# Two chained bottleneck blocks on one core: the column sums of the last stage spread over the units of a pair, a stream that takes no unit ahead, and one idle matmul more at two places of the Gram stages

## The chip, the cores and the metric

The kernel runs on one core of a Trainium2 chip. The metric is the time of one execution on the device in microseconds (us); less is better. In this text PE is TensorE, DVE is VectorE, ACT is ScalarE, POOL is GpSimd, and SP is SyncE, whose queue issues most of the DMAs.

## The reference

The input x is 64 images of 1024 channels and 14 x 14 pixels in float32. Two identical blocks follow each other. Each block computes

```
h = relu(bn1(conv1x1(x, w1) + b1))      # 1024 -> 256 channels
h = relu(bn2(conv3x3(h, w2) + b2))      # 256 -> 256
h = bn3(conv1x1(h, w3) + b3)            # 256 -> 1024
x = relu(x + softplus(residual_scale) * h)
```

where bn takes its mean and variance over all images and pixels. So no block can normalise before its whole convolution is done, and the work falls into stages.

## The kernel before, in words

**Stages.** In order of time the trace shows: the first 1x1 convolution (about 27 to 302 us), the 3x3 convolution of block 0 (302 to 592), the Gram stage of block 0 (from about 592), a fused stage that runs the last convolution of block 0 and the first of block 1 side by side (about 672 to 1270), the 3x3 convolution of block 1 (to 1562), its Gram stage (to about 1646), and the last stage (to the end at 1957.5), which is the last 1x1 convolution of block 1 with the residual sum, the relu and the output. In a Gram stage the variance of the third convolution is computed from the product of its input with itself, so that the convolution need not be run twice.

**Seven products.** A 1x1 convolution is done with seven products in place of eight for a 2 x 2 arrangement of weights and pixels. The class `Seven` names them `p1` to `p7`; behind each stands what is done with its result, `after1` to `after7`. They need four sums of the moving operand, `t1` to `t4`, and four of the weights. In the last stage a unit (`Conv3Pair`) is one choice q of 0 to 3 of output slots for two tiles of images, t and t + 1; four units make a pair of tiles, and there are 15 pairs (t = 1, 3, ..., 29). Each product there is one matmul call of 128x128 weights with 392 columns, which the trace shows as two instructions. The sums t1 to t4 depend on the pair only. They are the tiles `ct0` to `ct3`, made by `column_sums` (L423) in four DVE instructions: t3 (L430), t2 (L431, from t3), t1 (L432), t4 (L433, from t2). `ct0` and `ct1` (t1 and t2) have one buffer, `ct2` and `ct3` (t3 and t4) two.

**The order in a unit.** `stream` (L300) interleaves two units: p1 of the new unit, then p3 and p4 of the one before (`last`), then p6, p2, p5, p7 of the new one. After p2, p5, p3 and p4 DVE adds the scaled bank to the residual tile x (L466, banks named cx, cp, cp, cy). The bank cp that p5 starts is the same that p3 accumulates into, two products later, so p3 cannot start until the L466 after p5 has read the bank. After p1, p6 and p7 ACT saves the bank (L459, shown under its helper L333), and POOL adds these to x (L487, L513). `end` does three relus on ACT; `go_out` (L520) does the fourth relu on DVE (L522) and issues two output DMAs on SP (L525).

**The stream takes a unit ahead.** `stream` asks its generator for the following unit before it issues the present one. So what the generator does around a unit stands in the program one unit early: `go_out` of unit k - 2 and the loads of x (L123, behind unit q = 1 of a pair) stand ahead of unit k, and the column sums of the next pair stand ahead of unit q = 3 of the present one. The same `stream` serves the first stage (whose generator loads x) and the fused stage (loads of x and column sums).

**What sets the order on the engines.** Matmuls, ACT's instructions and some DVE instructions go through `tc.keep_in_program_order`, which pins an instruction behind the one that was traced last on its engine. The others are ordered when the program is built: each engine takes the earliest instruction in the program whose inputs and buffers are ready by a model. So an instruction that isn't pinned can be put ahead of its place in the program as soon as its buffer is free. L430 to L433 and L466 are not pinned; L522 is.

**Gram stages.** `conv2` ends with idle matmuls, `busy(psum, "m", 6)` (L968): matmuls with the identity of 448 columns into a bank that nobody reads. Behind them the Gram stage normalises the first pixels (ACT L546, DVE L552, L554, L994) and transposes them on PE in `by_tensor` (L1019, L1024).

Of the kernel before, what the change touches and what calls it, by code (L numbers as in the profile page):

```python
# [37 lines left out]
FP = mybir.dt.float32  # L38
# [3 lines left out]
P = 128  # L42
N, C, H, W = 64, 1024, 14, 14
HW = H * W
M = 256
CS = C // P
MS = M // P
G = 2
# [39 lines left out]
def bottlenecks(ctx: ExitStack, tc: tile.TileContext, x, w1s, w2s, w3s, pars, out):  # L88
# [14 lines left out]
    def two(t, s):  # L103

        j = t % (GI // G)
        return y_grp[:, s, t // (GI // G), :, j * G * W : (j + 1) * G * W]
# [63 lines left out]
    def busy(psum, tag, n, with_=None):  # L170

        v = ident if with_ is None else with_
        for i in range(n):
            matmul(psum.tile(448, tag), v, v[:, :1].to_broadcast([P, 448]), start=True, stop=True)
# [122 lines left out]
            yield from self.p3()  # L297
            yield from self.p4()

    def stream(items, beside=lambda: None):  # L300


        before, items = None, iter(items)
        now = next(items)
        while now is not None:
            following = next(items, None)
            yield from now.p1()
            if before is not None:
                beside()
                yield from before.last()  # L310
                beside()
            else:
                yield from now.p2()
            yield from now.p6()
            if before is not None:
                before.end()
                if following is not None:
                    beside()
                    yield from now.p2()
            beside()  # L320
            yield from now.p5()
            beside()
            yield from now.p7()
            beside()
            if following is None:
                yield from now.p2()
            before, now = now, following
        yield from before.last()
        before.end()

# [91 lines left out]

    def column_sums(pool, ys, n):  # L423

        sums = []
        for i in range(4):
            v = pool.tile([P, n], FP, tag=f"ct{i}", name=f"ct{i}", bufs=2 if i > 1 else 1)
            sums.append(v.rearrange("p (h l) -> p h l", l=G * W))
        t1, t2, t3, t4 = sums
        nc.vector.tensor_sub(t3, ys[1][1], ys[0][1])  # L430
        nc.vector.tensor_add(t2, t3, ys[0][0])  # L431
        nc.vector.tensor_sub(t1, ys[0][1], ys[0][0])  # L432
        nc.vector.tensor_sub(t4, ys[1][0], t2)  # L433
        return sums

    class Conv3(Seven):

# [118 lines left out]
    def conv2(psum, pool, b, par, aff, affine_of, stats):  # L556
# [395 lines left out]
        for k in range(NG * NF):  # L952
# [12 lines left out]
            item.columns(*qs)  # L965
            finished.send(item)
            queue = queue[1:] + list(itertools.islice(made, 1))
        busy(psum, "m", 6)  # L968

    def conv3(psum, t, o, w3, tag=None):  # L970
        ps = psum.tile(tag=tag)
# [6 lines left out]
    def gram(psum, pool, homes, aff, minus_c, beside):  # L978

        g0, g1 = psum.tile(M + 1, "cp"), psum.tile(P + 1, "ap")
        zts = [pool.tile([P, CH, M + 1], FP, tag=f"zt{i}", name=f"zt{i}") for i in range(NZT)]
        for zt in zts:
            nc.gpsimd.memset(zt[:, :, M:], 1.0)
        zts = itertools.cycle(zts)

        head = 3 * CH * P
        start = FIRST * CH * P
        bounds = [0, CH * P, head, head + STEP, *range(2 * GPX, NPX + 1, GPX)]  # L990
        pieces = list(zip(bounds, bounds[1:]))

        def less(s, y):
            tc.keep_in_program_order(nc.vector.tensor_scalar(y, y, minus_c[:, s : s + 1], None, ALU.add))  # L994

        def norm_to(end):

            while pieces and pieces[0][0] < end:
                a, e = pieces.pop(0)
                for s in reversed(range(MS)):  # L1000
                    y = y_all[:, s, a:e]
                    if a == 0 and s == 1:
                        norm_vector(s, y, aff, minus_c[:, s : s + 1])
                    else:
                        norm(s, y, aff)
                        less(s, y)

        def spread(k):

            first = start + k * STEP if k else head  # L1010
            norm_to(first + STEP)
            x = homes[k % 2][:, : MS * STEP].rearrange("p (s j f) -> p s j f", s=MS, j=4)
            for i, j in itertools.product(range(4), range(4)):
                queue = nc.gpsimd if 4 * i + j in (1, 3, 6, 8, 10, 13, 15) else nc.sync
                a = first + i * RUN
                queue.dma_start(out=x[32 * i : 32 * i + 32, :, j], in_=y_all[32 * j : 32 * j + 32, :, a : a + RUN])
            return x.rearrange("p s j f -> p (s j) f")

        def by_tensor(a):  # L1019
            tp = psum.tile(CH * M)  # L1020
            for c in range(CH):
                for s in range(MS):
                    tc.keep_in_program_order(
                        nc.tensor.transpose(  # L1024
                            tp[:, (c * MS + s) * P : (c * MS + s + 1) * P],
                            y_all[:, s, a + c * P : a + (c + 1) * P], ident,
                        )
                    )
            zt = next(zts)
            tc.keep_in_program_order(nc.vector.tensor_copy(zt[:, :, :M], tp.rearrange("p (c m) -> p c m", c=CH)))  # L1030
            return zt

        def by_vector(x, i):
            zt = next(zts)
            tc.keep_in_program_order(
                nc.vector.transpose(
                    zt[:, :, :M].rearrange("p b (n c) -> p b n c", c=32),
                    x[:, :, i * CH * 32 : (i + 1) * CH * 32].rearrange("p n (b r) -> p b n r", r=32),
                )
            )  # L1040
            return zt

        def pairs():

            norm_to(head)
            then = {
                1: lambda: ready.append(spread(0)),
                2: partial(norm_to, 2 * GPX),
                4: partial(norm_to, 3 * GPX),
                5: lambda: ready.append(spread(1)),  # L1050
            }
            for i in range(FIRST):
                a = i * CH * P
                yield by_tensor(a if a < head else a + STEP)
                if i in then:
                    then[i]()
            for k in range(STEPS):
                x = ready.pop(0)
                for i in range(RUN // (CH * 32)):
                    yield by_vector(x, i)  # L1060
                if k + 2 < STEPS:
                    ready.append(spread(k + 2))
            norm_to(NPX)
            for i in range(LAST):
                yield by_tensor(NPX - (LAST - i) * CH * P)

        ready = []
        total = NPX // (CH * P)
        before = None
        for k, zt in enumerate(itertools.chain(pairs(), (None,))):  # L1070
            if before is not None:
                for c in range(CH):
                    first, last = k == 1 and c == 0, k == total and c == CH - 1
                    matmul(g0, before[:, c, 0:P], before[:, c, :], start=first, stop=last)
                    matmul(g1, before[:, c, P:M], before[:, c, P:], start=first, stop=last)
            before = zt
            if k in beside:
                beside[k]()
        return g0, g1
# [61 lines left out]
    def final(psum, pool, xpool, xs, a, w3, aff):  # L1141


        units = []

        def pairs():
            for t in range(1, T - 1, 2):
                ys = [[two(t + i, s) for i in range(2)] for s in range(MS)]
                sums = column_sums(pool, ys, PX)
                for q in range(CS // 2):  # L1150
                    units.append(Conv3Pair(psum, pool, xs[t : t + 2], q, PX, ys, sums, w3, aff, out[t : t + 2]))
                    yield units[-1]

                    while len(units) > 2:
                        units.pop(0).go_out()
                    if q == 1:

                        for i in range(len(xs), min(t + 5, T)):
                            xs.append(load_x(xpool, 1, i))

        for _ in stream(pairs()):
            pass
        for unit in units:
            unit.go_out()
        residual(psum, xs[T - 1], 1, T - 1, a, aff)

    def fused(psum, pool, xpool, xs, w1, w3, aff, par, stats, one_done):
# [13 lines left out]
        def first_convs():  # L1181
            for t in range(T):
                yield Conv1(psum, pool, xs[t : t + 1], (t,), w1, par, stats, one_done)

        a, c = stream(first_convs()), stream(last_convs())
        for i in range(LAG):
            next(c)
        while True:
# [125 lines left out]
    with tc.tile_pool(name="first", bufs=1) as one, tc.tile_pool(  # L1314
# [32 lines left out]
                xs = [load_x(xpool, 0, t + i) for i in range(2)]  # L1347
                yield Conv1(psum, one, xs, (t, t + 1), w1, par[0], stats1, one_done)

        for _ in stream(items(), beside):  # L1350
            pass

    for b in range(2):
# [95 lines left out]
```

## Time and profile before

| | us |
|---|---|
| median of 3 runs | 1959.82 |
| lowest and highest | 1959.64, 1960.51 |
| profiled execution, whole | 1959.24 |
| its span, first to last instruction | 1957.5 |
| PE busy | 1919.9 (98%) |
| PEld busy | 1614.4 (82%) |
| DVE busy | 1552.4 (79%) |
| ACT busy | 1041.5 (53%) |
| POOL busy | 532.0 (27%) |
| DMA moved | 408.39 MB, 48.5% of 16 engines' time on SP's queue |

The busy times are summed over the whole span, whose stages have different limits, so a stage is read in a window of its own. A matmul's recorded length overlaps the next one's; the spacing of their starts is what PE needs. An instruction's line can be that of a helper (L168 for all matmuls, L333 for all pinned ACT instructions), so the tiles' names tell what it does. Between the span and the execution's time lie 1.74 us.

### The profile page before, as it was taken

The page shows a single profiled execution, that of the slowest core. Times are in us where ns is not written, and L with a number is a line of the kernel's source. Part 1 is how long each engine was busy: PE and PEld are TensorE (multiplying, and loading weights), DVE is VectorE, ACT ScalarE, POOL GpSimd, SP SyncE. Part 2 cuts the span into 40 slices and gives each one's busy share as a digit, 9 for nine tenths or more (in the row PEclk, how much of TensorE's full clock was granted, in tenths as well). Part 3 has the DMA queues.
Part 4 walks back from the last instruction along what each step waited for, and adds up shares of the span by engine and source line. Part 5 has one row for each costly group of instructions (what it writes and reads, how often), then busy time and mean ns, then how long its engine had stood idle before and what let it go on. Part 6 is the DMA issues. An engine that isn't in the chain of part 4 may idle for free.

```text
span 1957.5 us, 26989 instructions
## 1 busy us (share of the span) xinstructions
PE 1919.9 (98%) x9430; PEld 1614.4 (82%) x9430; DVE 1552.4 (79%) x2491; ACT 1041.5 (53%) x2082; POOL 532.0 (27%) x638
## 2 busy tenths in 40 slices
PE   9999999999999999999999999989999999999998
PEld 5555558999997799999999999989999887555554
DVE  5778768999998667676776776699999976888786
ACT  2222214677775055555555555457777641666665
POOL 0111100000105133433433333301010051666664
PEclk9999999999999999999999999999999999999999
DMA  7766635576747634444444444257667386899997
GB/s 289 278 248 254 249 112 165 178 208 191 207 142 203 198 135 187 173 165 177 182 169 165 179 184 166 99 183 204 203 192 207 124 199 232 298 322 339 336 341 264
DMA packets 188983, 408.39 MB, mean 209 GB/s; under 512 B 24944, under 2 KB 165136, under 8 KB 172336
## 3 DMA queue, kind: packets, MB, share of 16 engines
q1 hardware_dynamic: 161728, 324.66, 48.5%
q0 software_dynamic: 21504, 30.94, 6.9%
q10 hardware_dynamic: 5616, 51.06, 6.3%
q8 instruction: 75, 1.23, 0.3%
q14 instruction: 60, 0.49, 0.1%
HBM read 263.75 MB, written 115.34 MB: 194 GB/s over the span
## 4 chain that ended last, share of the span: by engine, by line
PE 90%; DVE 7%; issue 1%; ACT 1%; DMA 1%; SPq 0%; POOL 0%; DVEq 0%
PE ay L168 17%; PE cy L168 16%; PE columns L168 13%; PE cp L168 12%; PE ap L168 10%; PE m L168 6%; PE l L168 6%; PE ax L168 4%; PE cx L168 4%; PE ps L168 1%; DVE x L466 1%; DVE ct L431 1%; DVE f L801 0%; DMA home<-y 0%; DVE ct L433 0%
## 5 line engine op out<-in xcount | busy, mean ns | idle before, releaser
L333 ACT ACTIVATE cu<-cy,scale 128x196 f32<-128x196 f32 (+1 forms) x552 | 257.7, 473 | 286.7 <-PE cy L168 279.6
L168 PE MATMUL columns<-v,ub 128*128 128x224 f32 (+1 forms) x1536 | 301.1, 337 | 0.7 <-ACT columns L760 0.7
L168 PEld LDWEIGHTS columns<-v,ub 128*128 128x128 f32 x1536 | 269.4, 188 | 4.1 <-ACT columns L760 1.2
L333 ACT ACTIVATE x<-x,shift 128x392 f32<-128x392 f32 x428 | 239.7, 613 | 55.1 <-POOL x L492 53.2
L466 DVE SCALAR_TENSOR_TENSOR x<-cp,scale,x 128x196 f32<-128x196 f32 (+1 forms) x368 | 178.1, 484 | 98.0 <-PE cp L168 96.4
L168 PE MATMUL cy<-ct,ws 128*128 128x196 f32 (+1 forms) x736 | 222.0, 383 | 1.1 <-ACT cu L333 1.1
L168 PE MATMUL ay<-at,ws 128*128 128x196 f32 (+1 forms) x752 | 209.2, 381 | 0.0
L487 POOL TENSOR_TENSOR x<-x,cu 128x196 f32<-128x196 f32 (+1 forms) x184 | 159.2, 865 | 174.1 <-ACT cu L333 162.5
L492 POOL TENSOR_TENSOR x<-x,cu 128x392 f32<-128x392 f32 x124 | 125.9, 1015 | 192.8 <-DVE x L466 188.1
L168 PEld LDWEIGHTS ay<-at,ws 128*128 128x128 f32 x752 | 136.4, 190 | 33.6 <-ACT au L333 0.5
L168 PEld LDWEIGHTS cy<-ct,ws 128*128 128x128 f32 x736 | 133.4, 190 | 36.4 <-ACT cu L333 3.8
L168 PE MATMUL m<-sums,ua 128*128 128x224 f32 (+1 forms) x752 | 147.6, 340 | 6.2 <-DVE sums L624 6.2
L168 PE MATMUL l<-diffs,ub 128*128 128x224 f32 (+1 forms) x768 | 149.7, 338 | 3.0 <-PE columns L168 2.9
L513 POOL TENSOR_TENSOR x<-x,cu 128x392 f32<-128x392 f32 x120 | 124.5, 1038 | 86.1 <-DVE x L466 79.2
L871 POOL DMA_DIRECT2D y<-f x24 | 31.1, 1532 | 412.8 <-DVE f L801 320.8
L168 PEld LDWEIGHTS l<-diffs,ub 128*128 128x128 f32 x768 | 133.6, 189 | 7.0 <-PE columns L168 5.9
L168 PEld LDWEIGHTS m<-sums,ua 128*128 128x128 f32 x752 | 132.2, 191 | 8.7 <-DVE sums L624 7.9
L466 DVE SCALAR_TENSOR_TENSOR x<-cx,scale,x 128x196 f32<-128x196 f32 (+1 forms) x184 | 89.3, 485 | 59.1 <-PE cx L168 58.2
L333 ACT ACTIVATE au<-ay 128x196 f32<-128x196 f32 (+1 forms) x141 | 53.6, 380 | 152.0 <-PE ay L168 149.3
L168 PE MATMUL cx<-y,w 128*128 128x196 f32 (+1 forms) x404 | 124.1, 392 | 0.4 <-DVE x L1130 0.4
L168 PE MATMUL cy<-y,w 128*128 128x196 f32 (+1 forms) x404 | 123.8, 392 | 0.0
L168 PE MATMUL cp<-zt 128*128 128x257 f32 x392 | 118.8, 385 | 1.8 <-DVE zt L1030 1.7
(211 smaller groups left out, 3950.1 us busy)
## 6 DMA issues: line engine op xcount, KB each, us to landing
x<-in_x SPq DMA_DIRECT2D x62, 1568.0 KB, 6.8
ub<-u SPq DMA_DIRECT2D x94, 768.0 KB, 5.0
x<-mid SPq DMA_DIRECT2D x32, 1568.0 KB, 8.6
mid<-x ACTq DMA_DIRECT2D x31, 1568.0 KB, 5.1
out<-x SPq DMA_DIRECT2D x123, 392.0 KB, 6.5
ua<-u SPq DMA_DIRECT2D x94, 256.0 KB, 3.0
u<-y POOLq DMA_DIRECT2D x48, 256.0 KB, 5.9
home<-y SPq DMA_DIRECT2D x90, 96.0 KB, 4.2
```

What stands on the lines that cost most here:

```text
L168: tc.keep_in_program_order(nc.tensor.matmul(*args, **kw))
L333: tc.keep_in_program_order(nc.scalar.activation(*args, **kw))
L431: nc.vector.tensor_add(t2, t3, ys[0][0])
L466: nc.vector.scalar_tensor_tensor(v, bank, self.scale[:, o : o + 1], v, ALU.mult, ALU.add)
L487: nc.gpsimd.tensor_add(self.part(1, 1), self.part(1, 1), u3)
L492: nc.gpsimd.tensor_add(v, v, self.u12)
L513: nc.gpsimd.tensor_add(v, v, self.u12[:, i * self.n : (i + 1) * self.n])
L871: nc.gpsimd.dma_start(out=out_rows[0][:, o], in_=f[:, o], accum_op=ALU.add)
```

## The change

`stream` no longer asks for the following unit first; it is told the number of units, and takes each one when it is due. So everything that a generator does around a unit stands in the program behind the unit before it, one unit later than it did, in the first, the fused and the last stage.

In the last stage the four column sums are split from the allocation of their tiles (`sums_of`, `sum_steps`). The first pair's are made ahead of its units. Those of the next pair are made one at a time: t3 behind unit q = 0, t2 behind q = 1, t1 behind q = 2, t4 behind q = 3. All four tiles have two buffers there. `go_out` of unit k - 2 now stands behind the step of unit k, and the loads of x behind unit q = 1. The fused stage keeps `column_sums` and its buffers.

`conv2` ends with seven idle matmul calls instead of six, and one more stands behind the first `by_tensor` of each Gram stage, into the bank `ax`.

```
-        before, items = None, iter(items)
-        now = next(items)
-        while now is not None:
-            following = next(items, None)
+        before = None
+        for k, now in enumerate(items, 1):
             yield from now.p1()
...
-                if following is not None:
+                if k < total:
...
-            if following is None:
+            if k == total:
                 yield from now.p2()
-            before, now = now, following
+            before = now
...
+    def sums_of(pool, n, bufs=1):
+        tiles = [pool.tile([P, n], FP, tag=f"ct{i}", name=f"ct{i}", bufs=2 if i > 1 else bufs) for i in range(4)]
+        return [v.rearrange("p (h l) -> p h l", l=G * W) for v in tiles]
+    def sum_steps(ys, sums):
         t1, t2, t3, t4 = sums
+        return [
+            lambda: nc.vector.tensor_sub(t3, ys[1][1], ys[0][1]),
+            lambda: nc.vector.tensor_add(t2, t3, ys[0][0]),
+            lambda: nc.vector.tensor_sub(t1, ys[0][1], ys[0][0]),
+            lambda: nc.vector.tensor_sub(t4, ys[1][0], t2),
+        ]
...
-        busy(psum, "m", 6)
+        busy(psum, "m", 7)
...
                 yield by_tensor(a if a < head else a + STEP)
+                if i == 0:
+                    busy(psum, "ax", 1)
...
         def pairs():
+            def inputs(t):
+                ys = [[two(t + i, s) for i in range(2)] for s in range(MS)]
+                sums = sums_of(pool, PX, 2)
+                return ys, sums, sum_steps(ys, sums)
+            ys, sums, steps = inputs(1)
+            for step in steps:
+                step()
             for t in range(1, T - 1, 2):
-                ys = [[two(t + i, s) for i in range(2)] for s in range(MS)]
-                sums = column_sums(pool, ys, PX)
+                if t > 1:
+                    ys, sums, _ = following
+                following = inputs(t + 2) if t + 2 < T - 1 else None
                 for q in range(CS // 2):
                     units.append(Conv3Pair(psum, pool, xs[t : t + 2], q, PX, ys, sums, w3, aff, out[t : t + 2]))
                     yield units[-1]
+                    if following is not None:
+                        following[2][q]()
                     while len(units) > 2:
                         units.pop(0).go_out()
```

More of the change, by code (lines that the diff above doesn't have):

```diff
@@ L298, in last, with stream @@
             yield from self.p4()
-    def stream(items, beside=lambda: None):
-        before, items = None, iter(items)
-        now = next(items)
-        while now is not None:
-            following = next(items, None)
+    def stream(items, total, beside=lambda: None):
+        before = None
+        for k, now in enumerate(items, 1):
             yield from now.p1()
@@ L423, in column_sums @@
     def column_sums(pool, ys, n):
[L425 to L428, printed above, removed]
-        t1, t2, t3, t4 = sums
[L430 to L434, printed above, removed]
+        sums = sums_of(pool, n)
+        for make in sum_steps(ys, sums):
+            make()
+        return sums
+    def sums_of(pool, n, bufs=1):
+        tiles = [pool.tile([P, n], FP, tag=f"ct{i}", name=f"ct{i}", bufs=2 if i > 1 else bufs) for i in range(4)]
+        return [v.rearrange("p (h l) -> p h l", l=G * W) for v in tiles]
+    def sum_steps(ys, sums):
+        t1, t2, t3, t4 = sums
+        return [
[4 more added lines that the diff above has]
+        ]
     class Conv3(Seven):
@@ L1159, in pairs @@
                             xs.append(load_x(xpool, 1, i))
-        for _ in stream(pairs()):
+        for _ in stream(pairs(), (T // 2 - 1) * CS // 2):
             pass
@@ L1183, in first_convs @@
                 yield Conv1(psum, pool, xs[t : t + 1], (t,), w1, par, stats, one_done)
-        a, c = stream(first_convs()), stream(last_convs())
+        a, c = stream(first_convs(), T), stream(last_convs(), (T - 1) * CS // 2)
         for i in range(LAG):
@@ L1348, in items @@
                 yield Conv1(psum, one, xs, (t, t + 1), w1, par[0], stats1, one_done)
-        for _ in stream(items(), beside):
+        for _ in stream(items(), T // 2 - 1, beside):
             pass
```

## The prediction

> **What bounds the kernel now.** I read the page first, then the busy time by windows, then who waits for whom on PE, then the chain of work through the last stage. The page puts PE at 98% of the span, so only what leaves PE idle or slow can move the time. The change touches idle PE time in two places: the last stage and the start of the Gram stages. The waits of PE from 1640 us on are nearly one row:
>
> ```profile
> PE cp L168 <- DVE x L466: 6.1, 14, 0.4
> PE cy L168 <- ACT cu L333: 0.5, 1, 0.5
> ```
>
> Fourteen times, once between two pairs of tiles, p3 waits for the L466 that reads bank cp. The chain shows what made that L466 late:
>
> ```profile
> 1690.13 0.84 DVE ct L431
> 1690.98 0.02 issue
> 1691.00 0.57 DVE ct L433
> 1691.57 0.54 DVE x L466
> 1692.10 0.47 DVE ct L432
> 1692.58 0.55 DVE x L466
> 1693.12 0.04 issue
> 1693.17 0.93 PE cp L168 x2
> ...
> 1709.27 0.84 DVE ct L431
> ```
>
> Three column sums (t2, t4, t1) stand around the two L466 of unit q = 3. t1 and t2 have one buffer and can only be written once p5 and p6 of that unit have read the old ones. In the undisturbed units of this chain the spacing is 4.61 us (1696.73 to 1701.34), so four need 18.44; a pair takes 1709.27 - 1690.13 = 19.14. **The stall costs 0.70 us a pair**, more than the 0.43 in the row above because p3's weight load is then exposed too. Times 14: 9.8 us.
>
> DMA is the second limit there:
>
> ```profile
> 1709.30:1728.40 19.10, 18.67 (x57) 10.56 (x56) 15.50 (x24) 12.70 (x24) 12.41 (x13) 1.00 0.89 312
> ...
> 1804.90:1824.00 19.10, 18.67 (x57) 10.52 (x57) 15.51 (x25) 12.72 (x24) 12.41 (x13) 1.00 0.97 341
> ```
>
> (Columns: window, length, busy PE, PEld, DVE, ACT, POOL, PE clock, DMA share, GB/s.) DVE has 3.6 us free in a pair; the DMA engines are 89 to 97% occupied.
>
> At the two Gram starts the windows differ in the clock:
>
> ```profile
> 595.00:598.00 3.00, 3.00 (x12) 2.53 (x11) 2.58 (x4) 3.00 (x3) 0.00 (x0) 0.50 0.62 237
> ...
> 1565.00:1568.00 3.00, 3.00 (x21) 2.64 (x20) 2.59 (x4) 3.00 (x3) 0.00 (x0) 1.00 0.00 0
> ```
>
> In block 0 PE ran three microseconds at half clock, in block 1 not. From the first transposes to those of the fourth piece it took 593.48 to 600.89 = 7.41 us against 1563.49 to 1570.15 = 6.66.
>
> **What the Trainium skill says.** "SBUF — State Buffer", section "SBUF: two separate sides": POOL and a DVE instruction with two SBUF inputs, or one in a 2-port mode, take a shared pair of ports by an exclusive lock; whoever starts first blocks the other. The trace agrees: L432 takes 557 ns and L430 1372 ns when it meets POOL's L487 (1674.45 against 1674.28 to 1675.41, ending 0.41 later). "TensorE: Matmul & The Clock Gate", section "What's actually happening": an idle window of about 3.4 us halves PE's clock, and the window runs freely. The trace agrees with the half clock, and with the chance in it: two nearly equal gaps (1.19 and 0.67 us in block 0), one throttled. "Perfetto Trace Analysis", section "Engine Utilization": 358 GB/s of HBM per core; the trace shows 341 over a whole pair, near it.
>
> **The change, part by part.**
>
> *Idle matmuls.* One call is two instructions, 0.37 us apart: 0.75 us. The seventh fills 592.29 to about 593.04 of a gap that ends at 593.45, when the normalised pixels come. The one behind the first `by_tensor` fills about 593.92 to 594.7 of a gap that ends at 594.77 with DVE's L994. Cost nothing, or 0.1 if they overrun. Gain: 7.41 - 6.66 = 0.75 us where the throttle would fall, in none, one or both blocks of a run: 0 to 1.5; I take 0.75.
>
> *The stream in the first and fused stage.* No instruction is added. Loads of x stand one unit later in the program; they are not pinned and wait for a buffer anyway. In the first stage SP waits 138 us in sum for bank ap and 52 for ax to be read, so the load goes when the buffer is free. PE waits for no x there after 27 us. In the fused stage t1 and t4 now come behind the L466 of unit q = 3; PE waits there 2.1 us in 598, all at its start. I take 0, between -1 and +1.
>
> *go_out and the loads of the last stage.* L522 is now pinned behind the sum of the same unit, and with it two DMAs of L525 on SP, whose landing frees the buffer for the two loads L123 queued behind. Cover: the load issued at 1799.15 landed 6.9 us later, at 1806.0, and is first needed by the L466 after p5 at 1811.57. Of these 5.5 us the shorter pair takes 0.7, and 4.8 are left, against one unit of 4.61 at most. So nothing, but without reserve. For the last pair there is no next one: its L522 stand one unit later, and their DMAs (SP's L525 ends at 1946) stay ahead of the last outputs (to 1953): 0 to 0.5.
>
> *The sums.* The same 4 x 14 instructions, now with buffers of their own. A unit of DVE is 4 L466 at 0.54 spacing and one L522 (0.64 to 0.81), about 3 us of 4.61. There are two gaps: G1, 1.36 us between the L466 after p5 and the one after p3, in which L522 stands; and G2, 0.69 us ahead of the L466 after p2. L466 after p5 ends 0.34 us before its delay costs PE anything: 1.04 late made 0.70. One sum per unit (0.56 free, 0.82 to 1.37 against POOL) fits: in G1 L522 and the longest, t3, make 2.0 us; that is 0.65 late for the L466 after p3, and G2 takes it back. The trace shows exactly this in q = 0:
>
> ```profile
> 1673.89 0.64 DVE L522 TENSOR_SCALAR x<-x,shift 128x392 f32<-128x392 f32 x1
> 1674.45 1.37 DVE L430 TENSOR_TENSOR ct<-y 128x392 f32<-128x392 f32 x1
> 1675.75 0.61 DVE L466 SCALAR_TENSOR_TENSOR x<-cp,scale,x 128x392 f32<-128x392 f32 x1
> ```
>
> and no stall follows it. But these lines also warn: this t3 belongs to a pair after the next and stands three units ahead of its place. A sum with a free buffer isn't held back. If t2 then follows in G2 of the same unit, it must wait for POOL's L513 and the L466 after p5 comes about 0.67 late: 0.67 - 0.34 = 0.33. I expect a mixture and take 0.15 a pair, 0 to 0.33: 14 x (0.70 - 0.15) = 7.7 us gained, 5.2 to 9.8.
>
> *Ahead of the first unit* the second pair's t2, t1 and t4 can now be put into the chain of small instructions of the affine (1645.5 to 1649.5), which today holds five sums: 3 x 0.5 = 1.5 us later, mostly covered by PE's six banks of work until 1654; I take 0.4, 0 to 1.
>
> Sum: -0.75 - 7.7 + 0.4 = -8.05, made against the profiled execution's 1959.24 us, which lies 0.58 under the median. From the median: 1959.82 - 8.05 = **1951.8 us**.
>
> **The rivals.**
>
> *All sums gather in the first unit of the pair (slower).* At the end of unit q = 3 all buffers are free. If t1 and t3 both go into G1 of q = 0 with L522, POOL's L513 and L487 lock in between: G1 then starts at 0, L513 ends at 0.6, t1 at 1.0, L487 at 2.0, t3 at 2.4, L522 at 2.6. After the L466 of p3 and p4 (3.8), t2 waits for L513 (4.7) and the pinned L522 follows (5.0); the L466 after p5 ends at 6.06 instead of 4.69, 1.37 late: stall 1.03, or 1.3 with t4 there as well. It decides from 1.04 us of lateness on. 13 pairs x (0.33 to 0.6) = 4.3 to 7.8, less 0.7 for the first, less 0.75 for the clock, plus 0.4: +3.3 to +6.8, so 1963 to 1967. For it: L430's place, and nothing pins the sums. Against: L522 is pinned behind each of them, and the model that orders the queue need not see that much room.
>
> *The sums gather partly, and the change doesn't spread them (no change).* With one sum less in G1, or without the second L522, the stall comes out at 0.5 to 0.75: between -2.9 and +0.4 with the rest, so 1957 to 1960.
>
> *DMA becomes the bound.* A pair occupies the DMA engines for 0.89 to 0.97 of 19.1, on average about 18.1 us, hardly less than the 18.44 that PE wants; at that pace they would have to move 353 GB/s. If loads then land late, I put the floor at 18.7 to 18.9 a pair: 14 x 0.25 to 0.45 = 3.5 to 6 gained, 1953.5 to 1956. For it: the 97%. Against: the first load has 5.5 us in reserve, and DMA is emptier in the pairs before 1728 (89%).
>
> **How the numbers follow.** About 0.2% (3.9 us) is what a measurement of this kernel can tell from no change. Forecast (spread, stall under 0.33): 0.48, range 1949 to 1954.5. DMA: 0.14, of which nearly all is faster by over 0.2%. Partial gathering: 0.17, no change. Full gathering: 0.21, a few hundredths of it within 0.2%. So faster 0.61, within 0.2% 0.20, slower 0.19. The range leaves out the worst of the gathering and runs from everything going well (-9.8 - 1.5 + 0 = 1948.5) to 1965.
>
> **What would show it.** Right: L430 to L433 stand in four different units of a pair; the row PE cp <- DVE x L466 falls from 14 times to a few; the spacing of a pair is 18.44 to 18.8; the windows behind the first transposes show clock 1.00 in both blocks, with no new gap ahead of the second transposes. Wrong: two or more ct lines between the same two L466 of p5, with p3 waiting in q = 0's successor instead of q = 3's; or DVE's L466 waiting for DMA of x, with DMA share at 0.99; or L123 issued more than 4.8 us later behind the pair's start.

## Result and the profile after

| | before | after |
|---|---|---|
| median, us (5 runs each, same chip) | 1959.82 | 1969.31 |
| lowest to highest | 1958.33 to 1960.51 | 1967.72 to 1971.38 |
| profiled execution, whole / span | 1959.24 / 1957.5 | 1970.08 / 1968.3 |
| last stage: DVE's first copy of mv to the last matmul's end | 309.26 | 319.79 |

The ratio is 1.0049, with a 95% interval of 1.0035 to 1.0063. The change made the kernel **slower by about 9.5 us**; 1951.8 had been predicted. Of the 10.84 us between the two profiled executions, 10.53 lie in the last stage, and the stage starts 0.30 later. Of that, 0.28 are there already where the idle matmuls of block 0 begin (587.60 and 587.88 us). The profiles of this study reach the first transposes behind them anywhere from 592.0 to 593.9 us, so the 0.30 is not put down to the change.

Most lines of the code have moved by 7: L466 is now L473, L522 is L529, L525 is L532, POOL's L487 and L513 are L494 and L520, and the helper L333 is L331. t3, t2, t1 and t4 (L430 to L433) are L437, L438, L439 and L440. The waits of PE from 1640 us on, in us in total, times, and the longest:

```profile
PE cp L168 <- DVE x L473: 16.8, 13, 1.3
PE cy L168 <- ACT cu L331: 0.5, 1, 0.5
```

It is the same wait as before, p3 for the L473 that reads bank cp, but 1.3 long in place of 0.4. It comes 13 times and not 14. The second pair's sums are made ahead of the first unit, so the sums that gather between two pairs are always those of the pair after next; between the last two pairs, 14 and 15, there are none left to make, and nothing stalls. DVE's timeline around one such wait (start, length, instruction) shows what came ahead of it:

```profile
1692.69 0.62 DVE L473 SCALAR_TENSOR_TENSOR x<-cp,scale,x 128x392 f32<-128x392 f32 x1
1693.23 1.01 DVE L439 TENSOR_TENSOR ct<-y 128x392 f32<-128x392 f32 x1
1694.17 1.38 DVE L437 TENSOR_TENSOR ct<-y 128x392 f32<-128x392 f32 x1
1695.47 0.41 DVE L529 TENSOR_SCALAR x<-x,shift 128x392 f32<-128x392 f32 x1
1695.80 0.55 DVE L438 TENSOR_TENSOR ct<-ct,y 128x392 f32<-128x392 f32 x1
1696.28 0.61 DVE L473 SCALAR_TENSOR_TENSOR x<-cp,scale,x 128x392 f32<-128x392 f32 x1
1696.82 0.61 DVE L473 SCALAR_TENSOR_TENSOR x<-cy,scale,x 128x392 f32<-128x392 f32 x1
1697.35 1.06 DVE L440 TENSOR_TENSOR ct<-y,ct 128x392 f32<-128x392 f32 x1
1698.34 0.41 DVE L529 TENSOR_SCALAR x<-x,shift 128x392 f32<-128x392 f32 x1
1698.67 0.61 DVE L473 SCALAR_TENSOR_TENSOR x<-cx,scale,x 128x392 f32<-128x392 f32 x1
1699.20 0.61 DVE L473 SCALAR_TENSOR_TENSOR x<-cp,scale,x 128x392 f32<-128x392 f32 x1
```

The first line is the L473 after p5 of unit q = 3, the last that of unit q = 0 of the next pair. **All four sums stand between them**, three in G1 and one in G2, each gap with an L529. The steps that the program spreads over four units have gathered in one. From the one L473 to the other it is 1699.20 - 1692.69 = 6.51 us, where a unit without a stall takes 4.61: 1.90 late. Less the slack of 0.34 that the prediction read from the kernel before, 1.56 remain. The pairs confirm it: L437 comes every 19.99 us, 1.55 more than 18.44, where t3 came every 19.14. Of the increase, 13 x 0.85 = 11.05; the stall that is gone between the last two pairs gives 0.70 back; the rest of the stage's 10.53 is 0.18.

POOL's timeline in the same stretch shows what runs beside the sums:

```profile
1692.80 1.02 POOL L520 TENSOR_TENSOR x<-x,cu 128x392 f32<-128x392 f32 x1 [1.02 <-DVE x L473]
1694.04 1.08 POOL L494 TENSOR_TENSOR x<-x,cu 128x392 f32<-128x392 f32 x1 [0.22 <-ACT cu L331]
1696.97 1.02 POOL L520 TENSOR_TENSOR x<-x,cu 128x392 f32<-128x392 f32 x1 [1.85 <-DVE x L473]
```

Each of the three long sums begins while one of these adds runs and ends 0.42 to 0.43 us behind it (L439 at 1694.24, L437 at 1695.55, L440 at 1698.41). L438 meets none and takes 0.55.

The windows that answer those of before (window, length, busy PE, PEld, DVE, ACT, POOL, PE clock, DMA share, GB/s):

```profile
595.00:598.00 3.00, 3.00 (x20) 2.58 (x20) 2.58 (x5) 3.00 (x3) 0.00 (x0) 1.00 0.75 275
1565.00:1568.00 3.00, 3.00 (x21) 2.64 (x21) 2.58 (x4) 3.00 (x3) 0.00 (x0) 1.00 0.00 0
1709.30:1728.40 19.10, 17.81 (x55) 10.06 (x54) 14.96 (x24) 11.84 (x24) 11.41 (x12) 1.00 0.77 265
1804.90:1824.00 19.10, 17.80 (x55) 10.07 (x54) 15.22 (x24) 11.93 (x23) 11.55 (x12) 1.00 0.96 338
```

PE lacks 1.3 us in each of the last two, and DMA is less occupied than before, so DMA doesn't set the pace here. In the first window the clock is 1.00 where it was 0.50.

### The profile page after: what moved, and what is told of

The parts are those of the page before. It is cut to its first block, busy times and chain, and to the rows that moved or that the text cites. A ratio compares the mean times of both kernels' runs of the same rounds, so it can differ in the third digit from the quotient of the medians.

```text
span 1968.3 us, 27002 instructions
## 1 busy us (share of the span) xinstructions
PE 1921.9 (98%) x9438; PEld 1614.7 (82%) x9438; DVE 1548.1 (79%) x2491; ACT 1042.0 (53%) x2082; POOL 529.4 (27%) x638
## 4 chain that ended last, share of the span: by engine, by line
PE 76%; DVE 8%; DMA 7%; issue 5%; ACT 2%; POOL 1%; SPq 0%; DVEq 0%; POOLq 0%; ACTq 0%
PE ay L168 14%; PE cy L168 13%; PE columns L168 12%; PE cp L168 10%; PE ap L168 8%; PE m L168 6%; PE l L168 6%; DMA out<-x 5%; PE ax L168 4%; PE cx L168 4%; PE ps L168 1%; DVE x L473 1%; DMA home<-y 1%; ACT x L331 1%; POOL u L215 1%
## 5 line engine op out<-in xcount | busy, mean ns | idle before, releaser
L331 ACT ACTIVATE cu<-cy,scale 128x196 f32<-128x196 f32 (+1 forms) x552 | 256.7, 474 | 291.2 <-PE cy L168 285.4
L473 DVE SCALAR_TENSOR_TENSOR x<-cp,scale,x 128x196 f32<-128x196 f32 (+1 forms) x368 | 178.1, 484 | 129.3 <-PE cp L168 127.8
L331 ACT ACTIVATE x<-x,shift 128x392 f32<-128x392 f32 x428 | 241.0, 613 | 60.6 <-POOL x L499 53.0
L494 POOL TENSOR_TENSOR x<-x,cu 128x196 f32<-128x196 f32 (+1 forms) x184 | 158.6, 862 | 173.8 <-ACT cu L331 171.3
L520 POOL TENSOR_TENSOR x<-x,cu 128x392 f32<-128x392 f32 x120 | 122.0, 1018 | 100.1 <-DVE x L473 90.6
L331 ACT ACTIVATE au<-ay 128x196 f32<-128x196 f32 (+1 forms) x141 | 53.8, 382 | 155.3 <-PE ay L168 152.6
L168 PE MATMUL cp<-y,ws 128*128 128x196 f32 (+1 forms) x368 | 112.2, 386 | 17.6 <-DVE x L473 17.6
L473 DVE SCALAR_TENSOR_TENSOR x<-cx,scale,x 128x196 f32<-128x196 f32 (+1 forms) x184 | 89.2, 485 | 49.4 <-PE cx L168 47.8
```

Of the source, the lines that this page charges most:

```text
L168: tc.keep_in_program_order(nc.tensor.matmul(*args, **kw))
L331: tc.keep_in_program_order(nc.scalar.activation(*args, **kw))
L473: nc.vector.scalar_tensor_tensor(v, bank, self.scale[:, o : o + 1], v, ALU.mult, ALU.add)
L494: nc.gpsimd.tensor_add(self.part(1, 1), self.part(1, 1), u3)
L520: nc.gpsimd.tensor_add(v, v, self.u12[:, i * self.n : (i + 1) * self.n])
```

## Experiments

The theory: a sum that has a free buffer and isn't pinned is put ahead of its place in the program; the buffers of all four become free within about one unit, so they gather; and together they are long because POOL's adds block DVE's two-input instructions. Rivals: the second L529 among them, the new stream and its late loads, or a price of the sums wherever they stand. "Pair" is the spacing of t3 in the settled part of the profile, "stage" is as in the first table, "late" is the distance from one L473 (or L466) after p5 to the next, less 4.61, for the one that comes latest in a pair: unit q = 3 in before, stream_only and one_buffer, q = 0 of the next pair in the others.

| kernel | median, us | ratio to before, 95% | pair | stage | late |
|---|---|---|---|---|---|
| before | 1959.3 to 1959.8 | | 19.14 | 309.26 | 1.04 |
| after | 1969.31 | 1.0035 to 1.0063 | 19.99 | 319.79 | 1.90 |
| gram_only | 1958.92 | 0.9993 to 1.0009 | 19.14 | 309.32 | |
| two_buffers | 1964.61 | 1.0017 to 1.0038 | 19.60 | 314.55 | 1.50 |
| early_free | 1967.07 | 1.0025 to 1.0053 | 19.78 | 317.07 | 1.69 |
| no_pool | 1948.91 | 0.9935 to 0.9962 | 18.43 | 299.46 | 0.11 |
| stream_only | 1954.85 | 0.9968 to 0.9984 | 18.81 | 305.30 | 0.56 |
| pinned | 1957.10 | 0.9980 to 0.9993 | 18.43, later 19.5 to 19.8 | 306.07 | |
| early_pinned | 1949.12 | 0.9934 to 0.9961 | 18.43 | 299.47 | 0.00 |
| early_out_first | 1948.84 | 0.9934 to 0.9959 | 18.43 | 299.47 | 0.00 |
| one_buffer | 1974.94 | 1.0048 to 1.0107 | 20.31 | 325.91 | 1.86 |

pair = 18.44 + late - 0.34 holds within 0.02 us in before, after, two_buffers and early_free; in no_pool 0.11 lies under the slack of 0.34, and there is no stall. In stream_only and one_buffer the next unit adds some more (below).

**gram_only** (the kernel before with the idle matmuls)

```
-        busy(psum, "m", 6)
+        busy(psum, "m", 7)
...
+                if i == 0:
+                    busy(psum, "ax", 1)
```

> The kernel before with the two idle matmul calls alone; stream, sums and buffers as before. If the clock is the cause of the slow start of block 0's Gram stage, the window 595 to 598 shows clock 1.00 and the run is 0.75 us faster than before (1959.1), and no wait of PE is added. If the gain in the changed kernel's trace was chance, the time is that of before within 0.1. If the idle matmuls delay the transposes, it is 0.2 to 0.8 slower.

The window shows clock 1.00, and from the first transposes of block 0 to those of the fourth piece it took 6.66 us, 0.75 less than before. But the whole time can't be told from that of before: the medians differ by 0.5 us and the interval holds 1. A part of the gain is given back within the Gram stage. From the fourth piece to the first matmul of the fused stage it took 65.05 us, before 64.77; together 71.71 against 72.18. Over all profiles of this study, the eight with the added matmuls took 71.58 to 72.09 from the first transposes to the fused stage, 71.81 on average, the three without 72.02 to 72.42, 72.21 on average. So about 0.4 of the 0.75 stay on average, though the two groups overlap (72.09 and 72.02). What takes the rest wasn't tried.

**two_buffers** (all else as before)

```
-    def column_sums(pool, ys, n):
+    def column_sums(pool, ys, n, bufs=1):
...
-            v = pool.tile([P, n], FP, tag=f"ct{i}", name=f"ct{i}", bufs=2 if i > 1 else 1)
+            v = pool.tile([P, n], FP, tag=f"ct{i}", name=f"ct{i}", bufs=2 if i > 1 else bufs)
...
-                sums = column_sums(pool, ys, PX)
+                sums = column_sums(pool, ys, PX, 2)
```

> The kernel before with two buffers for t1 and t2 too; stream, the place of the sums in the program and the Gram stages as before. If free buffers alone make the sums gather, t3, t1 and t2 stand in one gap behind the L466 after p5 of unit q = 3, t4 in the next, and the stall rises above 0.70, to 0.9 to 1.3 a pair: 1962 to 1967. It is below the changed kernel's 1.55 because L522 isn't behind t4. If the loss comes from the new stream or from where the steps stand, the time stays at 1957 to 1960.

DVE's timeline (line numbers as before):

```profile
1690.54 0.62 DVE L466 SCALAR_TENSOR_TENSOR x<-cp,scale,x 128x392 f32<-128x392 f32 x1
1691.08 0.80 DVE L522 TENSOR_SCALAR x<-x,shift 128x392 f32<-128x392 f32 x1
1691.81 0.55 DVE L430 TENSOR_TENSOR ct<-y 128x392 f32<-128x392 f32 x1
1692.28 1.37 DVE L432 TENSOR_TENSOR ct<-y 128x392 f32<-128x392 f32 x1
1693.58 0.55 DVE L431 TENSOR_TENSOR ct<-ct,y 128x392 f32<-128x392 f32 x1
...
1695.12 1.06 DVE L433 TENSOR_TENSOR ct<-y,ct 128x392 f32<-128x392 f32 x1
1696.11 0.61 DVE L466 SCALAR_TENSOR_TENSOR x<-cx,scale,x 128x392 f32<-128x392 f32 x1
1696.64 0.61 DVE L466 SCALAR_TENSOR_TENSOR x<-cp,scale,x 128x392 f32<-128x392 f32 x1
```

Two more buffers and nothing else make the kernel about 5 us slower. With one buffer, t1 and t2 were held back until p5 and p6 of unit q = 3 had read the old ones; t2, t4 and t1 stood ahead of the L466 after p5 of that unit, and a t3 behind it. With free buffers all four gather behind that L466, ahead of the next unit's. Here L433 is followed by L466 at once; in the changed kernel an L529 stands between them. The lateness is 1.50 against 1.90.

**early_free** (the changed kernel)

```
-                    while len(units) > 2:
+                    while len(units) > 1:
                         units.pop(0).go_out()
-                    if q == 1:
+                    if q == 0:
```

> The changed kernel, its sums free, with go_out and the loads one unit earlier. DVE's queue then has t1, t3 and t2 in one gap without an L529 between them, and t4 with L529 in the next. If the second L529 among the sums is a part of the stall, it falls from 1.55 to 1.0 to 1.2 a pair, 1963 to 1966. If the sums alone make it, it stays at 1.5: 1968 to 1970. If the late loads made it, it falls to 0.7 or less.

A pair takes 19.78, a stall of 1.34: taking one of the two L529 out of the gaps is worth 0.21 a pair. That is less than expected, and 1967.07 lies above the 1963 to 1966; the second L529 is a part of the stall and not the main one. The early loads won nothing here, since DVE's waits in this stage name no load of x.

**no_pool** (the changed kernel; it leaves out POOL's adds in the last stage, so the saved results of p1, p6 and p7 are missing from its output there)

```
         def after3(self):
             self.add(0, 1, self.p)
-            for i in range(2):
-                v = self.part(0, i)
-                nc.gpsimd.tensor_add(v, v, self.u12[:, i * self.n : (i + 1) * self.n])
+
+        def after7(self):
+            self.saved(self.pool.tile([P, self.n], FP, tag="cu3", name="cu3", bufs=2), 1)
```

> The changed kernel without POOL's adds in the last stage (L494 behind p7, L520 behind p3 are left out, so two of the seven products are missing in part of the output); DVE's queue has the same order as the changed kernel. If the sums are long because POOL holds the shared port, t1, t3 and t4 take 0.55 each in place of 1.01, 1.38 and 1.06, about 1.5 is won of each pair's 1.55, and a pair takes 18.4 to 18.7 until the loads are late: 1949 to 1957. If the number of sums in the gap is what counts and not their length, it stays above 19.5: 1963 or more.

The same order on DVE, in its timeline:

```profile
1692.64 0.56 DVE L439 TENSOR_TENSOR ct<-y 128x392 f32<-128x392 f32 x1
1693.11 0.56 DVE L437 TENSOR_TENSOR ct<-y 128x392 f32<-128x392 f32 x1
1693.59 0.42 DVE L529 TENSOR_SCALAR x<-x,shift 128x392 f32<-128x392 f32 x1
1693.92 0.56 DVE L438 TENSOR_TENSOR ct<-ct,y 128x392 f32<-128x392 f32 x1
...
1695.47 0.56 DVE L440 TENSOR_TENSOR ct<-y,ct 128x392 f32<-128x392 f32 x1
1695.94 0.42 DVE L529 TENSOR_SCALAR x<-x,shift 128x392 f32<-128x392 f32 x1
```

From the start of L439 to that of the second L529 it is 3.30 us (1692.64 to 1695.94) where the changed kernel took 5.11 (1693.23 to 1698.34). Four sums and two L529 fit in two gaps if POOL isn't there: the stall is gone completely. **The stall needs both, the gathering and POOL's adds**; early_pinned below takes away the other one, with the adds in place. This kernel also settles a doubt: in the changed kernel the chain names an output DMA, landed at 1698.33, as what released the second L529. Here that L529 follows L440 after 0.47, there after 0.99, which is also what L433 takes in two_buffers, where no L529 follows it. So it is the length of t4 beside POOL that held the L529, and not the DMA.

**stream_only** (the kernel before with the new `stream`; sums as one block ahead of a pair's first unit)

```
-        before, items = None, iter(items)
-        now = next(items)
-        while now is not None:
-            following = next(items, None)
+        before = None
+        for k, now in enumerate(items, 1):
```

> The kernel before with the new stream alone: the four sums still stand as one block ahead of a pair's first unit, t1 and t2 with one buffer, and no idle matmuls. On DVE t2 and t4 stand ahead of the L473 after p2 of unit q = 3, t1 and t3 behind the L473 after p5. If only the sums ahead of the L473 after p5 cost time, t1's 0.47 leaves that place, and the stall falls from 0.70 to 0.2 to 0.4 a pair: 1953 to 1957. If sums behind it cost as much (t1 and t3 with L529 in one gap of 1.36), the stall is 0.7 to 1.2: 1960 to 1967. If the new stream costs the fused stage 0.65, that shows between 608 and 1563 us here.

This part of the change alone is a gain of 4.6 us. t2 and t4 stand ahead of the L473 after p5 of unit q = 3 and make it 0.56 late, for a stall of 0.22; t1 and t3 stand in G1 behind it (1.37 and 0.56) and make the next L473 0.15 late, which adds 0.15 to the pair (18.81 = 18.44 + 0.22 + 0.15). A sum behind that L473 is cheaper than one ahead of it: most of a unit is left to make it good. From the first matmul of the fused stage to the first of block 1's 3x3 convolution it took 610.01 us, as before (610.01), and 610.01 to 610.03 in every other kernel: the stream costs the fused stage nothing.

**pinned** (the changed kernel)

```
-                        following[2][q]()
+                        tc.keep_in_program_order(following[2][q]())
```

> The changed kernel with each sum step of the next pair pinned, so that one sum stands in each unit, ahead of L529, between the L473 after p5 and the one after p3. If the gathering is the whole loss, no p3 waits more than 0.1 for an L473, a pair takes 18.44 to 18.6, and the run takes 1949 to 1951. If DMA then sets the pace, 18.7 to 18.9 a pair: 1952 to 1956, with DVE waiting for x. If a sum costs PE its time wherever it stands, 19 a pair or more: 1958 or more.

Two of the expected answers came, one after the other. Until about 1809 us a pair takes 18.43 (18.26 to 18.72 in three of them): with one sum in a unit no p3 waits. Then a pair takes 19.5 to 19.8. Here are two windows, one row of DVE's waits, and the chain of work (start, length, what) of this kernel:

```profile
1775.40:1793.80 18.40, 18.40 (x57) 10.63 (x57) 17.32 (x25) 12.69 (x25) 12.37 (x13) 1.00 0.94 336
...
1832.00:1852.00 20.00, 19.18 (x59) 10.84 (x58) 17.40 (x25) 13.20 (x26) 12.71 (x13) 1.00 0.93 331
```

```profile
DVE x L473 <- DMA x<-mid: 4.6, 3, 1.7
```

```profile
1818.52 0.93 DVE ct L439
1819.44 1.10 DVE x L529
...
1820.60 0.54 SPq L532
...
1821.30 6.86 DMA x<-mid
...
1828.33 0.64 DVE x L473
```

A load landed at 1828.16 for which the L473 after p5 had waited 1.26 us. In the five pairs before it the landing was 0.2 to 0.8 us ahead of the L473, earlier 3.6 or more; in this one and the five behind it the L473 starts 0.1 to 0.2 us behind the landing. L529 stands behind a sum of 1.01 here and takes 1.17 itself, and one of its outputs stands ahead of the load on SP. The three loads before had gone out within 0.15 us of the landing of an output (1764.20, 1783.32 and 1801.36). The output in that place now landed at 1819.75, but the load went out only at 1821.30, behind the L532 of 1820.60, which waited for L529.

**early_pinned** (pinned with the diff of early_free) and **early_out_first** (that, and go_out ahead of the sum). The edit of the second:

```
+                    while len(units) > 1:
+                        units.pop(0).go_out()
                     if following is not None:
-                        following[2][q]()
-                    while len(units) > 2:
-                        units.pop(0).go_out()
-                    if q == 1:
+                        tc.keep_in_program_order(following[2][q]())
+                    if q == 0:
```

> Pinned, and go_out and the loads of x stand one unit earlier again, as in the kernel before (go_out of unit k - 1 behind unit k, loads behind q = 0). In pinned eight pairs took 18.43, then the p5 of q = 0 met an x that had not landed, and a pair took 19.5 to 19.8. If that was the loop of buffer, output and load, the loads are issued 4.6 earlier here, all pairs take 18.4 to 18.6 and the run takes 1948 to 1951. If it was the rate at which DMA moves the data (18.7 to 19.3 a pair), the loads fall behind again and the run takes 1952 to 1957.

> As early_pinned, with go_out ahead of the pinned sum in every unit, so that L529 doesn't wait for the sum and its outputs leave about 0.6 to 1.0 earlier. If the loop sets the pace this is as early_pinned or up to 3 better; if early_pinned already has 18.43 throughout, the two are equal within 1; if the rate of DMA sets it, both lie at 1952 to 1957.

Both have 18.43 in every settled pair to the end, and no p3 waits. The same bytes moved in less time, so the rate of DMA was not what held pinned at 19.5 to 19.8; the late place of the outputs and loads was. The two were moved together, and which of them counts wasn't tried. A smaller part of the rate isn't excluded: from 1793.8 to 1813.0 us, just ahead of pinned's first late load, the DMA engines were fully occupied (share 1.01, 362 GB/s). In early_out_first a load lands 4.1 us ahead of its use (1818.76, used by the second line below). **Of the kernels that compute the whole result, these two are the fastest**, 10.2 and 10.5 us below the kernel before, and can't be told apart. A unit on DVE and two windows of early_out_first:

```profile
1822.20 0.63 DVE L473 SCALAR_TENSOR_TENSOR x<-cx,scale,x 128x392 f32<-128x392 f32 x1 [0.69 <-PE cx L168]
1822.86 0.63 DVE L473 SCALAR_TENSOR_TENSOR x<-cp,scale,x 128x392 f32<-128x392 f32 x1
1823.40 0.80 DVE L529 TENSOR_SCALAR x<-x,shift 128x392 f32<-128x392 f32 x1
1824.12 0.55 DVE L437 TENSOR_TENSOR ct<-y 128x392 f32<-128x392 f32 x1
1824.83 0.63 DVE L473 SCALAR_TENSOR_TENSOR x<-cp,scale,x 128x392 f32<-128x392 f32 x1 [0.16 <-PE cp L168]
```

```profile
1738.00:1757.00 19.00, 19.00 (x59) 11.01 (x58) 15.37 (x25) 12.73 (x24) 14.00 (x13) 1.00 0.98 350
...
1872.00:1891.00 19.00, 19.00 (x59) 11.02 (x58) 15.00 (x25) 13.06 (x25) 13.98 (x13) 1.00 1.00 366
```

DVE is idle for 0.69 and 0.16 us in this unit. With go_out first, L529 takes 0.80 and the sum behind it 0.55, 1.35 together; in early_pinned they take 1.01 and 1.17. PE is busy for the whole of both windows.

**one_buffer** (the changed kernel)

```
-                sums = sums_of(pool, PX, 2)
+                sums = sums_of(pool, PX, 1)
```

> The changed kernel with one buffer for t1 and t2, as before. The sums can't gather: on DVE t2 has to wait for the p5 of unit q = 3 and t1 for its p6, and the L529 pinned behind t2, with its outputs and the loads queued behind them on SP, waits too. In the changed kernel a load is issued about 3 us behind a pair's start and has 10 in hand; here about 18 behind it, and landing 7 later it is about 6 late for the next pair's p5: 24 to 25 a pair and 2030 to 2050 in all. If the second buffers only made the sums gather and L529 isn't held, a pair takes 18.8 to 19.2 and the run 1953 to 1960.

A miss in size and in cause. L529 was held back as said, and the loads went out late (1790.12 and 1798.65, 1810.97 and 1819.31). But DVE waits for a load of x only once, 0.9 us, and in the settled pairs the loads land ahead of their use. The stall of 1.87 a pair is again a p3 behind an L473 (18.5 us in 15 waits of PE): the held L529 come out one behind the other among t2, t1 and t4 of unit q = 3, whose L473 after p5 is 1.86 late, and the next one 0.36 more. So an instruction that is pinned behind a step gathers too, when that step waits for a buffer.

## Why the prediction was wrong

**What bounds the kernel**: right. What changed the time lies where PE waits for the L473 of bank cp, and the 18.44 of a pair without a stall (18.43 measured), the 0.70 of before and the slack of 0.34 all held. Taking the stall away was worth 9.79 us of the stage (309.26 - 299.47, early_out_first); 9.8 had been read from the profile.

**The sums**: this is the step that failed. "I expect a mixture and take 0.15 a pair, 0 to 0.33" measured 1.55. It took the place of a step in the program for its place on the engine. The warning stood beside it: L430 three units ahead of its place. Nothing but the single buffers of t1 and t2 had separated the sums. With two buffers the old copies of all four are last read within about one unit, t2 by p6, t1 by p5 and t3 by p7 of unit q = 3, and t4 by its p4, which stands in the next unit; DVE made t1, t3, t2 and t4 there. That L522 is pinned behind each step, which the text held against the gathering, doesn't hold a sum back; it only drags L529 behind the gathered sums.

**The rival "All sums gather in the first unit of the pair"** is what happened; it had 0.21. Its mechanism is shown by two_buffers (the buffers alone make the sums gather), no_pool (the adds make them long) and early_pinned (apart they cost nothing). Its price was too low, 1.03 to 1.3 for 1.55. It had t1, t3 and the L522 in G1 and t2 with an L522 in G2, with t4 for 0.27 more; on the chip t2 stood in G1 as a third sum, and t4 with an L529 took G2. By the prediction's count G1 was to take 2.6 us; it took 3.05 (1693.23 to 1696.28). Most of the missing 0.53 of lateness, 1.90 for 1.37, is there. A stall of 1.55 in 13 pairs gives the stage 13 x 0.85 - 0.70 = 10.35 more. The 0.75 of the clock that the rival took off didn't show in the time. Hence 1969.3 and not 1963 to 1967. The prediction's range ended at 1965, because it left out the worst of the gathering.

**Idle matmuls**: right in the stage. From the first transposes to those of the fourth piece, the profiles with the added matmuls took 6.66 to 6.67 us and those without 7.25 to 7.50. That holds for block 0; block 1 took 6.66 to 6.68 in every profile, so in these runs the slow start fell in one block only, though the gaps ahead of it are nearly equal in both (1.19 and 0.67 us, 1.20 and 0.66 us before). Why it was always block 0 wasn't tried. No delay showed at that place. About 0.4 of the 0.75 is left at the end of the Gram stage, which the whole time can't show (gram_only).

**The stream in the first and fused stage**: 0 predicted, and 610.01 us in the fused stage with either stream (stream_only). From the first matmul to the first of block 0's 3x3 convolution the three profiles with the old stream took 303.70 to 303.94 us and the eight with the new one 303.73 to 304.21; a cost of about 0.2 there is neither shown nor excluded. That in the last stage the stream alone would win 4.6 us was not seen: the text costed only what it moves past, and not that the block of sums moves to another unit.

**go_out and the loads**: "nothing, but without reserve" was right and mattered only when the stall was gone. 4.8 against 4.61 leaves 0.2; in pinned the loads of five pairs landed 0.2 to 0.8 ahead of their use, and those behind them too late.

**DMA becomes the bound**: the rival's floor of 18.7 to 18.9 a pair did not hold. Two tiles in and two out, 4 x 1.606 MB in 18.43 us, are 348 GB/s, and early_out_first moved that to the end with PE fully busy. "Perfetto Trace Analysis", section "Engine Utilization", in the Trainium skill gives 358 GB/s of HBM per core as full use on trn2, and adds that this is the share when both cores of a pair use the memory and that one core alone can pull more. The runs of this kernel, on one core, agree: 366 GB/s in the second window of early_out_first, with no wait of PE. So the 341 that the prediction held against 358 was not near a limit that shows here, though at 350 and 366 the DMA engines were occupied for 0.98 and 1.00 of the time and had next to nothing to spare.

**Ahead of the first unit**: +0.4 predicted. Eight sums stand there after the change, five before, and yet the first L473 of bank cx comes 12.38 us behind the stage's start, as the first L466 did before. What the step cost later is at most the 0.18 left over in the stage.

## What to carry to other kernels

A second buffer takes away a wait, and with it the only thing that may have kept instructions apart; where an order is meant, pin it, and then read the engine's own timeline instead of the program's. When a stall is removed, ask which transfer was covered by it: here the gain of 9.8 us came whole only after the outputs and loads had been moved a unit forward in the program. Price an instruction by what runs beside it at its new place, not by its row.

## What was not expected of the hardware

In the changed kernel a sum on DVE took 0.55 us alone and 1.01 to 1.06 or 1.37 beside POOL's adds, with the same shapes; L529, with one tensor as input, took 0.41 to 1.20 in these runs. The Trainium skill, "SBUF — State Buffer", section "SBUF: two separate sides", states the lock between the two engines. The traces agree with it: each long sum ends 0.42 to 0.43 us behind an add of POOL. Without POOL's adds, and with the same order, the stretch of four sums and two L529 is 1.81 us shorter in each pair, and 20 us of the stage are gone (319.79 to 299.46).
